# A two-layer graph network: some gathered rows of the second layer become TensorE products, and x passes through DRAM between the layers

## The chip, the cores and the metric

The kernel runs on one core of a Trainium2 chip. The metric is the device time of one execution in microseconds. Engines are named as in the profile: PE is TensorE (PEld its weight loads), DVE is VectorE, ACT is ScalarE, POOL is GpSimd, and SP is SyncE, which here only issues transfers.

## The reference

A graph has 6,250 nodes with 128 features and 200,000 edges, sorted by target node. Two layers are applied, each on the normalised and rectified features, and each is added to x:

```python
h = jnp.maximum(_layernorm(x, axis=-1), 0.0)
x = x + _L0_gnn_ref(h, src, dst, ...)     # attention
h = jnp.maximum(_layernorm(x, axis=-1), 0.0)
x = x + _L1_gnn_ref(h, edge_attr_4, edge_attr_8, ...)   # messages
```

The first layer multiplies h by W, and for every edge takes the row of its source node, a logit per head, a softmax over the edges of each target, and the weighted sum. The second layer multiplies h by `wup` to a table of 128 columns (s and v parts), takes for every edge the table's row of the source node, multiplies it by weights which a small network (8 to 64 to 64 to 128) makes from the edge's features, forms 256 message values and sums them per target; `wout` maps the sums back to 128.

## The kernel before

Edges are cut into 1,563 tiles of 128 edges, one edge per partition. KB = 16 tiles make a block; there are NB = 98 blocks, the last with 11 tiles. Nodes are cut into NX = 50 tiles of 128; a block of edges feeds some 64 nodes, so that a node tile is finished by every second block. A function at run time checks that the targets are even enough, and `even_edges` (line 1008) does the work; `tile_any_edges` is not entered.

**Gathers.** The rows of source nodes come by indirect DMA, one per tile, issued by POOL (`gather`, line 831, issue on line 833): table t0 (136 columns) in the first layer, t1 (128 columns) in the second. A block's rows lie in one buffer `g` of `z_pool`, which has 5. POOL issues them in program order and runs ahead as far as the buffers allow; `take_rows` asks for a block's rows two blocks ahead in the second layer.

**Row transfers.** In blocks 3, 6, 9, ..., 93 (`by_row`) the last tile is not gathered: SP issues 128 transfers of one row each, whose offsets it loads from `at` (`rows_by_row`, lines 1117 to 1133), into one of 3 buffers `r`; `filled` (line 1142) copies it into `g` on ACT. `rows_until` places these transfers in SP's program about three blocks ahead of their use.

**First layer.** For each block DVE, PE and ACT make one-hot matrices, logits, maxima and weights, and PE sums the rows by matrix products (`sums`, line 1284). When a node tile is ended, `node_x` to `node_s` (lines 1298 to 1341) add it to x, normalise and multiply by `wup`, and ACT leaves the table's tile in `sv` (2 buffers). `node_out` (line 1343) stores it from SP to t1 and to t1z, a copy of t1 without the last NL = 3 node tiles. x stays in SBUF, in `x_all`, 50 tiles.

**Change of layers.** The first NE = 24 tiles of the second layer are gathered from t1z, before the last three node tiles are known; PE adds those nodes' rows with one-hot products (`late_ends`, `late_rows`, lines 1658 and 1672). The first gather from t1 waits for the store of the last node tiles.

**Second layer.** A step is 4 tiles. In each, PE does a quarter of the next block's network (`network`, line 1553) and the weights of the next step (`tensor_weights`), DVE forms the messages (`messages`, line 1592, from `vy` to `mj`) and the next one-hot matrix, and PE sums (`sums1`, line 1617). Every second block PE, ACT and DVE finish a node tile (`node1`, line 1625) and SP stores it (`node_out1`). `edge_rows` (line 1545) loads the edge features `ft` and `yb` from SP two blocks ahead. PE, DVE, ACT and SP work in the order of the program; on each of them an instruction that waits holds all behind it.

The one-hot comparison reads the column numbers from PSUM (`held`), where also copies of three columns of `yb` lie, in turn for three blocks.

Of the kernel before, what the change touches and what calls it, by code (L numbers as in the profile page):

```python
# [9 lines left out]
F32 = mybir.dt.float32  # L10
# [731 lines left out]
def tile_even_edges(  # L742
# [88 lines left out]
    def gather(to, table, tiles, width, first=0):  # L831
        for k, t in enumerate(tiles, first):
            nc.gpsimd.indirect_dma_start(  # L833
                out=to[:, k, :width], out_offset=None, in_=table,
                in_offset=bass.IndirectOffsetOnAxis(ap=src_col[:, t : t + 1], axis=0))
        return to
# [171 lines left out]
def even_edges(tc, v):  # L1008
# [8 lines left out]
    with ExitStack() as ctx:  # L1017
        z_pool = ctx.enter_context(tc.tile_pool(name="fz", bufs=5))
        const = ctx.enter_context(tc.tile_pool(name="fconst", bufs=1))
        s_pool = ctx.enter_context(tc.tile_pool(name="fs", bufs=16))  # L1020
        row_pool = ctx.enter_context(tc.tile_pool(name="frow", bufs=3))
        of_l0 = ctx.enter_context(ExitStack())
        l0c = of_l0.enter_context(tc.tile_pool(name="l0c", bufs=1))
# [15 lines left out]
        x_all = const.tile([P, NX, P], F32, name="fx_all")  # L1039
# [3 lines left out]
        identb = l0c.tile([P, P], BF, name="fidentb")  # L1043
        nc.vector.tensor_copy(identb, ident)
# [50 lines left out]
        a3p = const.tile([P, 2, P], F32, name="fa3p")  # L1095
        nc.sync.dma_start(a3p, v["a3p"])
# [4 lines left out]
        wout = const.tile([P, 2, P], F32, name="fwout")  # L1101
        nc.sync.dma_start(wout, v["wout"])
# [5 lines left out]
        with tc.tile_pool(name="fat_ps", bufs=1, space=PSUM) as at_ps:  # L1108
            col = l0c.tile([P, P], F32, name="fcol")
            n = NB - 1  # L1110
            nc.vector.tensor_copy(col[:, :n], v["src_col"][:, KB - 1 : n * KB : KB])
            p_c = at_ps.tile([P, P], F32, name="p_c")
            nc.tensor.transpose(p_c[:n], col[:, :n], ident)
            for i, w in enumerate((ZW, P)):
                nc.vector.tensor_scalar(at[i][:n], p_c[:n], float(4 * w), None, op0=OP.mult)
# [30 lines left out]
        def one_hot(t, m, iota=iota):  # L1146

            s = s_pool.tile([P, 4, P], F32, name="s")
            nc.vector.tensor_tensor(s[:, :m], iota[:, None, :].to_broadcast([P, m, P]),  # L1149
                                    dloc[:, t : t + m].unsqueeze(2).to_broadcast([P, m, P]),  # L1150
                                    OP.is_equal)
            return s

        def finish(b, p_u, width, carry, agg, pool):

            if b % 2 == 0:
                agg = pool.tile([P, MW], F32, name="agg")
            o = agg[b % 2 * WB : b % 2 * WB + WB, :width]
            if carry is None:
                nc.vector.tensor_copy(o, p_u[:WB, :width])  # L1160
            else:
                nc.vector.tensor_add(o, p_u[:WB, :width], carry[:, :width])
            carry = pool.tile([WB, MW], F32, name="carry")
            nc.scalar.copy(carry[:, :width], p_u[WB:, :width])
            return carry, agg

# [5 lines left out]
        with tc.manual_schedule(engines=in_order), \  # L1172
# [116 lines left out]

            def node_rows(i, n):  # L1290
                nc.sync.dma_start(x_all[:, i : i + n, :],
                                  xp[i * P : (i + n) * P].rearrange("(j p) f -> p j f", p=P))

            def with_bias(i, n):
                x_i = x_all[:, i : i + n, :]
                nc.vector.tensor_add(x_i, x_i, bias_b[:, None, :].to_broadcast([P, n, F]))

            def node_x(u):
                i, n, agg = u["i"], u["n"], u["agg"]
                x_i = x_all[:, i : i + n, :]  # L1300
                if n == 1:
                    with_bias(i, n)
                rd = l0n.tile([P, 2, H], F32, name="rd")[:, :n]
                nc.vector.tensor_scalar(rd, agg[:, :n, F:ZW], 1e-9, None, op0=OP.max)
                nc.vector.reciprocal(rd, rd)
                sums_ = agg[:, :n, :F]
                heads = sums_.rearrange("p j (h d) -> p j h d", d=D)
                nc.vector.tensor_mul(heads, heads, rd.unsqueeze(3).to_broadcast([P, n, H, D]))
                nc.vector.tensor_add(x_i, x_i, sums_)
                u["mv"] = moments(l0n, x_i, n, f"n{n}")  # L1310
# [4 lines left out]
            def node_h(u):  # L1315
                i, n = u["i"], u["n"]
                rs, mr = normal(l0n, u["mv"], u["rs"], n, f"n{n}")
                xn = u["xn"] = l0n.tile([P, 2, P], F32, name="xn")
                nc.scalar.activation(xn[:, 0, :], x_all[:, i, :], AF.Identity, bias=mr[:, 0, :],
                                     scale=rs[:, 0, :])  # L1320
                if n == 2:
                    nc.vector.tensor_scalar(xn[:, 1, :], x_all[:, i + 1, :], u["mv"][:, 1, 0:1],
                                            rs[:, 1, :], op0=OP.subtract, op1=OP.mult)
# [19 lines left out]
            def node_out(u):  # L1343
                i, n, sv = u["i"], u["n"], u["sv"]
                first = i * P - W0
                for table in (t1, t1z) if i < LATE else (t1,):
                    if i == 0:
                        nc.sync.dma_start(table[: P - W0, :], sv[W0:, 0, :])
                    else:
                        nc.sync.dma_start(  # L1350
                            table[first : first + n * P].rearrange("(j p) f -> p j f", p=P), sv)

# [59 lines left out]
            rows, rows_until.n, late = rows_by_row(0, t0, ZW), 0, []  # L1412
            for i in range(2):
                node_rows(i, 1)
            for g in range(NG - 3):
# [3 lines left out]
                for n in late:  # L1419
                    node_out(n)  # L1420
                if g % 2 == 0 and g // 2 + 2 < NX - 2:
                    node_rows(g // 2 + 2, 1)
# [10 lines left out]
                maxima(c)  # L1433
                ends_of(n2, 1)
# [33 lines left out]
                late = nodes  # L1468
                if b4:
                    sums(b4, 8)  # L1470
                if g == NG - 4:
                    for q in range(4):
                        ends_of(c1, q)
                    masks_of(c1)
                    for q in range(4):
                        turned(c1, q)
                        er_of(c1, q)
                    er_sum(c1, True)
            node_rows(NX - 2, 2)
            for n in late:  # L1480
                node_out(n)
            with_bias(NX - 2, 2)
# [5 lines left out]
            maxima(c3)  # L1488
            neighbours(c4, c5, c3)
# [26 lines left out]
            (u,) = ended(c4, st)  # L1516
            weighted(c2, 0)
# [22 lines left out]
        with tc.manual_schedule(engines=in_order), \  # L1540
                tc.tile_pool(name="l1", bufs=3) as l1, \
                tc.tile_pool(name="l1n", bufs=2) as l1n, \
                tc.tile_pool(name="l1_ps", bufs=2, space=PSUM) as l1_ps:

# [8 lines left out]
            def network(b, step):  # L1553
# [7 lines left out]
                if step == 3 or 2 * q0 + 8 >= KT[b] and second:  # L1561
                    c["yp"] = held[:, P + b % 3 * KB * 3 : P + (b % 3 + 1) * KB * 3].rearrange(
                        "p (t i) -> p t i", i=3)
                    nc.scalar.copy(c["yp"], c["yb"][:, :, 1:4])  # L1564
# [59 lines left out]

            def node1(i, agg):
                x_i = x_all[:, i, :]
                p_n = l1_ps.tile([P, 4, P], F32, name="p_n", bufs=1)
# [3 lines left out]
                nc.scalar.copy(m_t, p_n[:, :2])  # L1631
                for q in range(2):
                    nc.tensor.matmul(p_n[:, 2, :], m_t[:, q, :], wout[:, q, :], start=q == 0, stop=q == 1)
                nc.vector.scalar_tensor_tensor(x_i, p_n[:, 2, :], POST, x_i, op0=OP.mult, op1=OP.add)
                return i

            def node_out1(i):
                x_i = x_all[:, i, :]
                if i == 0:
                    nc.sync.dma_start(out[: P - W0, :], x_all[W0:, 0, :])  # L1640
# [5 lines left out]
            iota_p = held[:, :P]  # L1646
# [25 lines left out]
            def late_rows(t):  # L1672
                if t < NE:
                    z, k0, oh = blk[t // KB]["z"], t % KB, late_ends.of.pop(t)
                    p_n = l1_ps.tile([P, 4, P], F32, name="p_n", bufs=1)
                    for k in range(4):
                        for j in range(NL):
                            nc.tensor.matmul(p_n[:, k, :], oh[:, j, k, :], sv_late[:, j, :],
                                             start=j == 0, stop=j == NL - 1)
                    z = z[:, k0 : k0 + 4, :P]  # L1680
                    nc.vector.tensor_add(z, z, p_n)
# [6 lines left out]
            def take_rows(b):  # L1688
# [3 lines left out]
                elif b < NB:  # L1692
                    blk[b]["z"] = gathered(t1, range(b * KB, b * KB + KT[b] - (b in by_row)), P)

            rows, rows_until.n, late = rows_by_row(1, t1, P), 0, []
# [9 lines left out]
            us[0]["s"] = one_hot(0, us[0]["m"], iota_p)  # L1705
# [3 lines left out]
            for i, u in enumerate(us):  # L1709
                b, k0, m = u["b"], u["k0"], u["m"]  # L1710
                if k0 == 0:
                    take_rows(b + 2)
                    filled(1, b, blk[b]["z"], P)
                    edge_rows(b + 2)
                if k0 == 4:
# [8 lines left out]
                messages(u)  # L1724
                late_rows(4 * (i + 1))
                if i + 1 < NU:
                    n = us[i + 1]
                    n["s"] = one_hot(n["b"] * KB + n["k0"], n["m"], iota_p)
# [18 lines left out]
            p_n = l1_ps.tile([P, 4, P], F32, name="p_n", bufs=1)  # L1747
# [11 lines left out]
            x_i = x_all[:, NX - 2 :, :]  # L1759
# [140 lines left out]
```

## Time and profile before

| what | value |
|---|---|
| median of 3 runs (lowest to highest) | 3866.83 us (3866.21 to 3874.36) |
| profiled execution, whole | 3867.01 us |
| its span, first to last instruction | 3865.1 us |
| first layer / second layer | to about 1962 us / from there |
| busy share PE, DVE, ACT, POOL | 73, 58, 36, 75% |
| granted PE clock, mean | 0.813 |
| DMA engines busy | about 0.28 in the first layer, 0.24 in the second |

Times within the trace are microseconds from the start of the span. A row of the groups gives line, engine, operation, output and input by name, count, busy time, mean of one in ns, and behind the second bar the idle time of the engine just before such instructions with what ended most of it. In a list in order of time the columns are start, length (of all merged, with their number behind x), engine, line, and in brackets the idle time before with what ended it. "issue" is a time in which the engine waited for nothing that the profile shows.

### The profile page before, as it was taken

What the parts mean: (1) busy time and instruction counts of PE and PEld (TensorE: products, weight loads), DVE (VectorE), ACT (ScalarE), POOL (GpSimd) and SP (SyncE); (2) the same over time, 40 slices, a digit from 0 to 9 for tenths busy, and PEclk for the clock granted to TensorE, in tenths of its full rate; (3) what the DMA queues carried; (4) which work ended last, traced back from release to release, by engine and by line L of the source; (5) the groups of instructions that cost most, each with busy time, mean ns of one, the idle gap of its engine ahead of it and who ended that gap; (6) DMA issues with size and microseconds to landing.
All of it is one profiled execution on the core that took longest, in us unless ns stands there. A gap on an engine that the chain in (4) does not pass through costs nothing. (4 is left out here: it accounts for less than half of the span.)

```text
span 3865.1 us, 62861 instructions
## 1 busy us (share of the span) xinstructions
PE 2825.6 (73%) x14836; PEld 2380.3 (62%) x14836; DVE 2237.5 (58%) x5485; ACT 1403.0 (36%) x3625; POOL 2900.2 (75%) x3074
## 2 busy tenths in 40 slices
PE   4666566666666666666688888888887788888777
PEld 3666566666566656656576666666665666666655
DVE  6555444444444444444457777777766666666666
ACT  3333322232323233322324444444444444444443
POOL 6777777777777777777777777777777777777776
PEclk7676666666666666666689999999999999999999
DMA  6222222222222222222222222222222222222221
GB/s 176 60 64 62 65 64 62 65 64 63 63 64 63 64 62 65 62 64 62 62 60 62 62 62 62 62 63 62 61 63 62 62 62 62 62 61 62 61 61 50
DMA packets 192048, 250.91 MB, mean 65 GB/s; under 512 B 78768, under 2 KB 141872, under 8 KB 191664
## 3 DMA queue, kind: packets, MB, share of 16 engines
q0 software_dynamic: 98048, 207.21, 22.6%
q1 hardware_dynamic: 93184, 39.50, 3.9%
q8 instruction: 120, 1.97, 0.2%
q14 instruction: 264, 2.16, 0.2%
q10 hardware_dynamic: 432, 0.08, 0.0%
HBM read 232.98 MB, written 13.25 MB: 64 GB/s over the span
## 5 line engine op out<-in xcount | busy, mean ns | idle before, releaser
L833 POOL DMA_INDIRECT g<-ft,fsrc x3024 | 2857.7, 945 | 934.4 <-issue 859.1
L1622 PE MATMUL p_u<-mj,s 128*128 128x256 f32 x3126 | 793.6, 398 | 211.2 <-DVE mj L1614 209.8
L1622 PEld LDWEIGHTS p_u<-mj,s 128*128 128x128 f32 x3126 | 591.1, 196 | 379.4 <-DVE mj L1614 303.3
L1286 PE MATMUL p_u<-g,s 128*128 128x136 f32 x3062 | 588.1, 372 | 1.0 <-DVE g L1281 0.4
L1286 PEld LDWEIGHTS p_u<-g,s 128*128 128x128 f32 x3062 | 563.2, 276 | 1.7 <-DVE g L1281 1.6
L1589 ACT ACTIVATE p_w<-p_w,yb 128x64 f32<-128x64 f32 x1563 | 450.3, 288 | 120.5 <-PE p_w L1585 78.8
L1605 DVE TENSOR_TENSOR vy<-g,p_i 128x384 f32<-128x384 f32 x387 | 213.0, 550 | 364.6 <-DMA g<-ft,fsrc 258.1
L1585 PE MATMUL p_w<-fa3p,h 128*128 128x256 f32 x1564 | 412.3, 387 | 0.0
L1203 PE MATMUL p_d<-fident,s 128*128 128x128 f32 x1563 | 370.6, 400 | 0.9 <-DVE s L1149 0.9
L1585 PEld LDWEIGHTS p_w<-fa3p,h 128*128 128x128 f32 x1564 | 289.3, 195 | 117.9 <-issue 51.9
L1228 DVE TENSOR_TENSOR e_s<-g,p_n 128x128 f32<-128x128 f32 x96 | 27.5, 286 | 554.6 <-DMA g<-ft,fsrc 498.1
L1570 ACT ACTIVATE h<-p_h,fb 128x512 f32<-128x512 f32 x196 | 134.7, 687 | 580.2 <-PE p_h L1568 580.2
L1203 PEld LDWEIGHTS p_d<-fident,s 128*128 128x128 f32 x1563 | 300.7, 218 | 11.6 <-DVE s L1149 1.1
L1196 ACT COPY mk<-p_m 128x385 f32<-128x385 f32 (+1 forms) x99 | 47.7, 482 | 701.4 <-PE p_m L1193 693.6
L1281 DVE TENSOR_TENSOR g<-g,pe 128x1024 f32<-128x1024 f32 x193 | 225.5, 1209 | 127.3 <-ACT g L1272 127.3
L1205 ACT CAST d<-p_d 128x512 bf16<-128x512 f32 x391 | 228.2, 586 | 180.4 <-PE p_d L1203 137.2
L1231 PE MATMUL pe<-fident,e_s 128*128 128x128 f32 x98 | 37.7, 384 | 329.9 <-DVE e_s L1229 329.9
L1149 DVE TENSOR_TENSOR s<-p_n,fdloc 128x512 f32<-128x512 f32 x391 | 266.1, 682 | 7.2 <-ACT sv L1341 3.4
L1149 DVE TENSOR_TENSOR s<-p_i,fdloc 128x512 f32<-128x512 f32 x391 | 266.4, 681 | 3.8 <-ACT p_i L1564 3.8
L1568 PE MATMUL p_h<-ft,fa1p 128*128 128x128 f32 x1568 | 215.4, 282 | 67.7 <-DMA ft<-in_e_f_dram 67.7
L1568 PEld LDWEIGHTS p_h<-ft,fa1p 128*128 128x128 f32 x1568 | 209.2, 196 | 88.6 <-issue 72.4
L1575 ACT ACTIVATE h<-p_h,fb 128x512 f32<-128x512 f32 x196 | 134.7, 687 | 304.4 <-PE p_h L1572 304.4
(213 smaller groups left out, 3345.6 us busy)
## 6 DMA issues: line engine op xcount, KB each, us to landing
r<-ft SPq DMA_DIRECT2D x3968, 0.5 KB
r<-ft SPq DMA_DIRECT2D x3968, 0.5 KB
g<-ft,fsrc POOLq DMA_INDIRECT x3024
ft<-in_e_f_dram SPq DMA_DIRECT2D x98, 64.0 KB
yb<-in_e_y_dram SPq DMA_DIRECT2D x98, 32.0 KB
fx_all<-in_e_xp_dram SPq DMA_DIRECT2D x48, 64.0 KB
out_dram<-fx_all SPq DMA_DIRECT2D x47, 64.0 KB
ft<-sv SPq DMA_DIRECT2D x46, 64.0 KB
```

Source lines behind the costliest of these rows:

```text
L833: nc.gpsimd.indirect_dma_start(out=to[:, k, :width], out_offset=None, in_=table, in_offset=bass.IndirectOffsetOnAxis(ap=src_col[:, t : t + ...
L1149: nc.vector.tensor_tensor(s[:, :m], iota[:, None, :].to_broadcast([P, m, P]), dloc[:, t : t + m].unsqueeze(2).to_broadcast([P, m, P]), OP. ...
L1203: nc.tensor.transpose(p_d[:, k, :], c["s"][q][:, k, :], ident)
L1205: nc.scalar.copy(d[:, :m], p_d[:, :m])
L1281: nc.vector.tensor_mul(zh, zh, p_a[:, k0 : k0 + m].unsqueeze(3).to_broadcast([P, m, H, D]))
L1286: nc.tensor.matmul(c["p_u"][:, :ZW], c["s"][k // 4][:, k % 4, :], c["z"][:, k, :], start=c["o"] + k == 0, stop=c["o"] + k == KT[c["b"]] - 1)
L1568: nc.tensor.matmul(p_h[:, q, :], a1p[:, q0 + q, :], c["ft"], start=True, stop=True)
L1570: nc.scalar.activation(c["h1"], p_h, AF.Silu, bias=b1)
L1585: nc.tensor.matmul(w[:, k : k + n].rearrange("p k a u -> p (k a u)"), c["h2"][q // 4][:, q % 4, :], a3p[:, :n].rearrange("p k f -> p (k f) ...
L1589: nc.scalar.activation(w[:, k, ::2, :], w[:, k, ::2, :], AF.Copy, scale=c["yb"][:, k0 + k, 0:1])
L1605: nc.vector.tensor_mul(vy, v_n, y_p)
L1622: nc.tensor.matmul(blk[b]["p_u"][:, :MW], u["s"][:, k, :], u["mj"][:, k, :], start=k0 + k == 0, stop=k0 + k == KT[b] - 1)
```

## The change

In the second layer, the 21 blocks 10, 14, 18, ..., 90 (`dense1`) no longer gather tile 14 (KD). Its rows are made by PE: the table is kept in SBUF as three bf16 parts whose sum is the f32 value (`t1s`, 50 node tiles x 3 x 128), the node numbers of the tile's edges are compared with those of NR = 17 node tiles at once (`dense_ends`: one PE product, two DVE comparisons into the bf16 matrix `ohs`), 51 products are summed in PSUM for three ranges of nodes (`dense_rows`: 12 in each of the last two steps of the block before, 9 in each of the first three of the block itself), and DVE takes the right range for each edge (`dense_taken`, three operations, into the tile's place in `g`).

To make room in SBUF, `x_all` goes. In the first layer a node tile's x and the table's three parts lie in one buffer of 5; DVE makes the parts (`parts`: two casts, two subtractions per tile, one block after the table's tile), and SP stores both in one transfer of 160 KB to `x1` in DRAM (`parts_out`, a block after `node_out`). The last three tiles store x alone. The second layer loads x again per node tile (`node_rows1`, 64 KB) and the parts in 8 transfers, one in each of blocks 0 to 7 (`table_tiles`); the last three tiles' parts come from `sv_late` in SBUF.

With it go: a3p and wout are loaded at the start of the second layer instead of the first; `node1` works in `held`; `yp` alternates between two blocks; the first layer's one-hot matrices have their own pool, the second's a pool of 5; `fcol` lies in a pool of its own; an unused `identb` goes; once, in block 4 of the first layer, `ends_in_ranges` makes the node numbers and range marks for the dense tiles.

```diff
-        x_all = const.tile([P, NX, P], F32, name="fx_all")
...
+        dense1 = set(range(10, NB - 4, 4))
...
+        def in_three(to, of, rest):
+            to = [to[..., k, :] for k in range(3)]
+            nc.vector.tensor_copy(to[0], of)
+            nc.vector.tensor_sub(rest, of, to[0])
+            nc.vector.tensor_copy(to[1], rest)
+            nc.vector.tensor_sub(to[2], rest, to[1])
...
+            def parts(u):
+                i = u["i"]
+                if i < LATE:
+                    rest = l0n.tile([P, P], F32, name="rest", bufs=1)
+                    in_three(parts_of(row_of[i][:, 0]), u["sv"][:, 0], rest)
+            def parts_out(u):
+                i = u["i"]
+                if i < LATE:
+                    nc.sync.dma_start(x1[i], row_of[i][:, 0])
...
+            def node_rows1(i, n=1):
+                x_i = x_of[i] = l1n.tile([P, n, P], F32, name=f"x{n}", bufs=4 if n == 1 else 1)
+                nc.sync.dma_start(x_i, x1[i : i + n, :, :P].rearrange("j p f -> p j f"))
...
+            def table_tiles(b):
+                i = 6 * b
+                if i < LATE:
+                    n = min(6, LATE - i)
+                    nc.sync.dma_start(t1s[:, i : i + n].rearrange("p j s f -> p j (s f)"),
+                                      x1[i : i + n, :, P:].bitcast(BF).rearrange("j p f -> p j f"))
+            def dense_ends(b):
+                p_x = blk[b]["p_x"] = l1_ps.tile([P, 4, P], F32, name="p_x", bufs=1)
+                nc.tensor.matmul(p_x[:, 3, :], key[:, b : b + 1].to_broadcast([P, P]), ident,
+                                 start=True, stop=True)
+                oh = blk[b]["oh"] = l1d.tile([P, NR, P], BF, name="ohs")
+                for k, n in ((0, half), (half, NR - half)):
+                    nc.vector.tensor_tensor(
+                        oh[:, k : k + n], p_x[:, 3:4, :].to_broadcast([P, n, P]),
+                        place_r[:, k : k + n].unsqueeze(2).to_broadcast([P, n, P]), OP.is_equal)
+            def dense_rows(b, k0, n):
+                c = blk[b]
+                for k in range(k0, min(k0 + n, NR)):
+                    i = order[k]
+                    m = len(range(i, NX, NR))
+                    for s in range(3):
+                        nc.tensor.matmul(c["p_x"][:, :m, :], c["oh"][:, k, :], t1s[:, i::NR, s, :],
+                                         start=k == 0 and s == 0, stop=k == NR - 1 and s == 2)
+            def dense_taken(b):
+                c = blk[b]
+                z = c["z"][:, KD, :P]
+                nc.vector.tensor_scalar(z, c["p_x"][:, 0, :], part[:, b, 0:1], None, op0=OP.mult)
+                for r in (1, 2):
+                    nc.vector.scalar_tensor_tensor(z, c["p_x"][:, r, :], part[:, b, r : r + 1], z,
+                                                   op0=OP.mult, op1=OP.add)
+            def dense_step(b, q):
+                if b + 1 in dense1:
+                    if q == 1:
+                        dense_ends(b + 1)
+                    elif q > 1:
+                        dense_rows(b + 1, (q - 2) * 4, 4)
+                if b in dense1:
+                    dense_rows(b, 8 + 3 * q, 3)
+                    if q == 2:
+                        dense_taken(b)
...
                 elif b < NB:
-                    blk[b]["z"] = gathered(t1, range(b * KB, b * KB + KT[b] - (b in by_row)), P)
+                    blk[b]["z"] = gathered(t1, [k for k in range(b * KB, b * KB + KT[b])
+                                                if not (b in by_row and k % KB == KB - 1)
+                                                and not (b in dense1 and k % KB == KD)], P)
...
                     edge_rows(b + 2)
+                    if b % 2 == 0:
+                        node_rows1(b // 2, 1 if b < NB - 2 else 2)
+                    table_tiles(b)
...
                 messages(u)
+                if i == 26:
+                    in_three(t1s[:, LATE:], sv_late, rest)
+                dense_step(b, k0 // 4)
                 late_rows(4 * (i + 1))
```

## The prediction

> **What bounds the kernel now.** I read the page's busy rows first, then the groups, then the gather queue in order of time, then the waits.
>
> ```profile
> PE 2825.6 (73%) x14836; PEld 2380.3 (62%) x14836; DVE 2237.5 (58%) x5485; ACT 1403.0 (36%) x3625; POOL 2900.2 (75%) x3074
> ...
> PEclk7676666666666666666689999999999999999999
> ```
>
> No engine is over 75% busy, and the TensorE clock is 0.65 in the first layer and near full in the second. So the busy shares settle nothing.
>
> ```profile
> L833 POOL DMA_INDIRECT g<-ft,fsrc x3024 | 2857.7, 945 | 934.4 <-issue 859.1
> L1622 PE MATMUL p_u<-mj,s 128*128 128x256 f32 x3126 | 793.6, 398 | 211.2 <-DVE mj L1614 209.8
> ```
>
> POOL's idle time is "issue": it waited for nothing. TensorE waits for messages. In order of time, across the change of layers, the gathers run without a break:
>
> ```profile
> 1956.22 0.94 POOL L833 DMA_INDIRECT fz_first<-ft1z,fsrc  x1 [0.30 <-issue]
> 1957.47 0.94 POOL L833 DMA_INDIRECT g<-ft1z,fsrc  x1 [0.30 <-ACT fsv_late L1341]
> ...
> 1966.20 0.94 POOL L833 DMA_INDIRECT g<-ft1z,fsrc  x1 [0.30 <-issue]
> 1967.45 0.94 POOL L833 DMA_INDIRECT g<-ft,fsrc  x1 [0.30 <-issue]
> ```
>
> One gather starts every 1.249 us (1957.47 to 1967.45 is 8 steps). From 65 us to the last one at 3849.48 there are 3,031 starts, on average 1.2489 us apart, in both layers alike, and 15.6 us of work follow. POOL sets the end.
>
> What stands second? Second layer, waits:
>
> ```profile
> DVE vy L1605 <- DMA g<-ft,fsrc: 258.1, 159, 3.7
> ...
> PE p_h L1568 <- DMA ft<-in_e_f_dram: 67.7, 29, 4.9
> ```
>
> The waits for gathers all fall after 2790 us. The waits of TensorE for `ft` nearly all fall before it. Until then the consumers lag behind the gathers and are paced by SP, whose queue holds the row transfers:
>
> ```profile
> 2035.10 0.37 SPq L1549 DMA_DIRECT2D ft<-in_e_f_dram  x1
> 2035.53 0.42 SPq L1551 DMA_DIRECT2D yb<-in_e_y_dram  x1
> 2036.05 16.41 SPq L1130 DMA_DIRECT2D r<-ft  x44
> 2052.56 0.37 SPq L1549 DMA_DIRECT2D ft<-in_e_f_dram  x1
> ```
>
> SP issues the `ft` of block 3 at 2035.10 and that of block 43 at 2768.68: 18.34 us a block. POOL needs 15.67 x 1.249 = 19.57. So the lag shrinks, by 1.2 us a block. It starts at 34.7 us (block 2 is begun at 2032.06, its gathers ended at 1997.4), and five gather buffers allow about 54 before POOL must stop.
>
> **The change, part by part.** *Removed gathers.* Blocks 10, 14, ..., 90 are 21; each loses one gather: 21 x 1.249 = **26.2 us** off POOL's queue.
>
> *TensorE.* Per dense block 51 bf16 products (48 of 384 columns, 3 of 256), and one f32 product. No row has 384 columns. Nearest: three bf16 products of 512 columns and one of 128, weights reloaded each time, took 0.86 us (L923), the last alone about 0.23, so 0.21 each or 0.41 ns a column: 0.16 us for 384. Four bf16 pairs with 128x128 weights but 24 columns took 0.27 us (L1214), so a weight load adds at most 0.03. Lower end 51 x 0.16 = 8.2 us, upper end (unoverlapped, 0.45 us each as in row L1193) 23. I take 8.8, by the L923 row, plus 0.2.
>
> *VectorE in the second layer.* Two comparisons of 1,152 and 1,024 elements (row L1281, 1,024 in 1.21 us): 2.55; three 128-wide takes, 0.65 back to back. 3.2 us a dense block.
>
> *Does this fit?* Four blocks need 64 - 1.33 (row transfers) - 1 = 61.6 gathers, 76.9 us. The consumers' best pair of blocks (2032.06 to 2065.35) took 33.3, partly waiting for SP; without those waits about 32.3, so 64.6 for four. With 9.0 of TensorE and some 0.5 of VectorE that is not overlapped: about 74. SP: 4 x 18.34 plus two loads of x at 0.47: 74.3. Since each waits for the other in turn, I take 75 for the pair. That is under 76.9, so POOL stays the bound, by only 2.5%.
>
> *What SP gets to wait for.* Each store of x waits for VectorE's parts of that tile; they are made in the block before, ahead of what SP waits for there anyway. `fcol` is copied only after the early rows' last copies, which delays the first row transfer by 0.25 us.
>
> *SP, second layer, once.* Eight loads of the table's parts (576 KB each) and the moved a3p and wout. The 838 KB `fd_q` and 1.5 MB around it landed within 11 us at the start, about 200 GB/s; so a table load lands after some 5 us, while SP tolerates about eight issues (3.3 us) behind an unfinished one. 0.5 to 3.5 us of SP each; I take 2.5, 20 in all, and 4 at the change of layers. This delays `ft` and the rows behind it, so the consumers; the lag at block 10 becomes about 45 instead of 25, still under 54. From there it shrinks by (76.9 - 75)/4 a block, 39 us up to block 90, and by some 3 us a block in the last seven, where SP has no rows left and no dense block comes. It must be down by 57 to cost nothing (in the steady state it is -12); I get 60. So hidden, by little.
>
> *SP, first layer.* 47 stores of 160 KB and one load more or less for the tail. An issue takes 0.4 to 0.5 whatever its size (408 KB: 0.38). SP needs 36.0 us for two blocks (212.6 to 500.6 in eight steps), POOL 39.1; the store makes it 36.5. Its early lag of some 65 us behind the node work now lasts until about 1330 us instead of 1180; POOL does not wait for it, as the first row transfers are late by 10 us and the buffers are freed with 14 us to spare.
>
> *First layer, VectorE.* Two casts and two subtractions for each of 47 tiles, about 0.25 us each, on an engine that is under half busy. The price could lie elsewhere. The Trainium skill ("SBUF — State Buffer", Who interferes with whom) says that VectorE and GpSimd share a port pair by an exclusive lock, which casts within SBUF and operations with two SBUF inputs can take. The trace does show it, for long operations:
>
> ```profile
> 53.38 0.94 POOL L833 DMA_INDIRECT g<-ft,fsrc  x1 [0.30 <-issue]
> 54.63 2.56 POOL L833 DMA_INDIRECT g<-ft,fsrc  x1 [0.30 <-issue]
> 57.50 1.49 POOL L833 DMA_INDIRECT g<-ft,fsrc  x1 [0.30 <-issue]
> ```
>
> ```profile
> 54.49 1.89 DVE L1067 TENSOR_TENSOR feq<-fd_q 128x1664 f32<-128x1664 int32 x1 [10.42 <-DMA fd_q<-in_e_dstt_dram]
> 56.30 1.89 DVE L1070 TENSOR_TENSOR feq<-fd_q,fnxt 128x1664 f32<-128x1664 int32 x1
> ```
>
> Four such operations of 1.9 us cost POOL 3.2 us. By the rule each of 188 new ones could hold it for its length: 188 x 0.25 = 47 us, and the change would lose (3888). But short ones leave no mark: six single-input operations within SBUF at 43.1 to 44.1 fall on gathers of 0.94 and 0.95, and the first layer, with some 240 two-input operations of 0.3 us (L1229, L1296, L1308, L1309), has the second layer's step (1.2490 against 1.2489). I take 0 to 6 us, 0.5.
>
> *Change of layers.* The first gather from t1 (1967.45) needs the late rows' store, issued at 1962.15. Now VectorE does 0.8 us more ahead of it, and a3p, wout and five loads stand in front of it on SP (7 x 0.45). They can go while ScalarE still works on those rows. 0 to 3 us; I take 1.5.
>
> **Sum:** -26.2 + 0.5 + 1.5 + 0.7 for what the lag may leave = -23.5. The profiled execution took 3867.0 (span 3865.1 and 1.9 around it), 0.2 from the median 3866.8. Likeliest: **3843 us**, its own range 3839 to 3850.
>
> **Rivals.**
> *The lag is not recovered* (chance 0.22). If SP and the consumers need 75.8 instead of 75 for four blocks, they win back 20.25 x 1.1 + 21 = 43 of the 57, and 14 us lengthen the tail: 3857; between 75.2 and 76.2, 3845 to 3865. For it: three queues within 3%. [...]
> *The second layer's consumers become the bound* (0.10; the slower side). Place: TensorE's queue in the 21 dense blocks. Price: every microsecond on four blocks costs 20.25 at the end, once the 2.5 of reserve are gone. It is even with before at 76.3, that is with 0.20 us a product instead of 0.17 if none of it is overlapped, and 78 gives 57 - 21 + 22 = 58 us of tail, 3901. For it: TensorE is 83% busy there. Against: the L923 row.
> *The port lock* (0.06): 3870 to 3888, as above.
> *No gain, because the gathers removed were not pacing* (0.03): 3867. The unbroken 1.249 us steps speak against it.
>
> **Numbers.** The likeliest has 0.59. Below 3859.1 is faster by over 0.2% (what this measurement can just tell): 0.59 and just over half of the first rival, 0.71. Within 0.2%: the rest of it, most of the fourth and a little of the second, 0.14. Slower: 0.15. The range reaches from the likeliest's lower end through the first rival: 3838 to 3867.
>
> **What would show it.** Right: 3,003 gathers of this group at 1.249 us steps with no other gap over 1 us; TensorE busier in the second layer by some 190 us of columns; the tail after the last gather near 16 us. Wrong: gathers of 1.1 us and more in the first layer (port), a wait of POOL at 1960 to 2250 (SP's table loads, buffers), a tail of 25 us or more (lag), waits of VectorE for gathers gone altogether (consumers bound).

## The result, and the profile after

The changed kernel took **3843.01 us**, the median of four runs (3841.60 to 3843.57); the kernel before, on the same chip, 3866.52 us (3866.13 to 3874.36). The ratio is 0.9934 with a 95% interval of 0.9917 to 0.9951, so it is faster by 0.66%; by the medians it is 23.5 us, or 0.61%, because one of the four runs before took 3874.36. The profiled execution took 3843.54 us, with a span of 3841.8.

The page of the changed kernel: busy rows, granted TensorE clock, and the two groups that were shown of before.

```profile
PE 2965.8 (77%) x15949; PEld 2484.1 (65%) x15949; DVE 2355.1 (61%) x5805; ACT 1405.7 (37%) x3625; POOL 2880.8 (75%) x3053
...
PEclk7676766666666666666679999999999999999999
...
L834 POOL DMA_INDIRECT g<-ft,fsrc x3003 | 2838.2, 945 | 928.5 <-issue 853.5
L1701 PE MATMUL p_u<-mj,s 128*128 128x256 f32 x3126 | 764.1, 388 | 88.7 <-DVE mj L1693 86.5
```

There are 3,003 gathers instead of 3,024, of the same 945 ns, and their idle time is still "issue". TensorE is busy 140 us longer, and its wait for messages ahead of `p_u` fell from 211.2 to 88.7 us: dense products stand where it used to wait. Part of the fall is the lag's: e1, told below, has no dense product and still waits 139.4 instead of 209.8 us there for VectorE.

The last gather, before and then in the changed kernel:

```profile
3849.48 0.94 POOL L833 DMA_INDIRECT g<-ft,fsrc  x1 [0.30 <-issue]
...
3824.22 0.94 POOL L834 DMA_INDIRECT g<-ft,fsrc  x1 [0.30 <-issue]
```

The last gather starts at 3824.22 instead of 3849.48, so 25.3 us earlier; 17.5 us of work follow it, counted from its start, instead of 15.7. That makes 23.4 us of span. POOL still sets the end.

The waits of the whole execution, for the rows that told the consumers' state before (total us, times, longest):

```profile
DVE vy L1684 <- ACT p_i L1643: 79.5, 94, 3.3
PE p_h L1647 <- DMA ft<-in_e_f_dram: 59.7, 39, 4.9
...
DVE vy L1684 <- DMA g<-ft,fsrc: 21.2, 14, 2.9
```

Before, VectorE waited 258.1 us for gathers in this place (line L1605 there). Now its largest wait here is another one, and 21.2 us in 14 waits are left of it. The consumers (TensorE, VectorE and ScalarE, which work on what POOL gathers) lag behind the gathers nearly to the end. SP's queue shows the pace that they are given. The `ft` of block 11 and that of block 91:

```profile
2195.22 0.36 SPq L1628 DMA_DIRECT2D ft<-in_e_f_dram  x1
...
3684.41 0.37 SPq L1628 DMA_DIRECT2D ft<-in_e_f_dram  x1
```

1489.19 us for 80 blocks are 18.615 a block, 74.46 for four.

A table of the lag (when VectorE begins a block's messages, less when the block's last gather ended, in us; about -13 is the steady state of a kernel whose consumers wait for gathers), worked out from the times of both engines, with the span from the start of the last gather to the end. It takes in the experiments, which are told below.

| kernel | block 10 | 30 | 50 | 70 | 90 | 96 | last gather starts | work after it |
|---|---|---|---|---|---|---|---|---|
| before | 25 | 4 | -12 | -12 | -12 | -13 | 3849.48 | 15.7 |
| after | 43 | 32 | 14 | 3 | -8 | -13 | 3824.22 | 17.5 |
| e1: no dense block | 40 | 20 | -1 | -12 | -12 | -13 | 3851.35 | 17.3 |
| e2: every third block | 43 | 46 | 52 | 55 | 54 | 45 | 3816.24 | 67.6 |
| e3: table loads twice | 59 | 43 | 26 | 15 | 5 | -11 | 3829.54 | 16.2 |
| e6b: one more load a block on SP | 46 | 45 | 39 | 36 | 35 | 19 | 3823.16 | 41.8 |
| e7b: a third more products | 42 | 30 | 15 | 4 | -7 | -13 | 3824.11 | 15.2 |
| e9: one in three, all even | 42 | 36 | 21 | 14 | 3 | -10 | 3814.36 | 15.2 |
| e10: one in four, odd | 40 | 39 | 38 | 37 | 37 | 28 | 3823.75 | 51.1 |

### The profile page after: what moved, and what is told of

Read it like the earlier page. It is cut to its first block, busy times and chain, and to the rows that moved or that the text cites. A ratio compares the mean times of both kernels' runs of the same rounds, so it can differ in the third digit from the quotient of the medians.

```text
span 3841.8 us, 65586 instructions
## 1 busy us (share of the span) xinstructions
PE 2965.8 (77%) x15949; PEld 2484.1 (65%) x15949; DVE 2355.1 (61%) x5805; ACT 1405.7 (37%) x3625; POOL 2880.8 (75%) x3053
## 5 line engine op out<-in xcount | busy, mean ns | idle before, releaser
L1701 PE MATMUL p_u<-mj,s 128*128 128x256 f32 x3126 | 764.1, 388 | 88.7 <-DVE mj L1693 86.5
L1701 PEld LDWEIGHTS p_u<-mj,s 128*128 128x128 f32 x3126 | 581.2, 192 | 216.1 <-DVE mj L1693 139.0
```

What stands on the lines that cost most here:

```text
L1701: nc.tensor.matmul(blk[b]["p_u"][:, :MW], u["s"][:, k, :], u["mj"][:, k, :], start=k0 + k == 0, stop=k0 + k == KT[b] - 1)
```

## The experiments

The theory from the two traces: the 21 gathers are the whole gain; what decides whether it arrives at the end is the lag, and the lag shrinks at the pace that SP's queue allows. The rivals: other edits had a part in the gain; TensorE, not SP, sets the consumers' pace.

**e1: no dense block.** Is the gain that of the gathers?

```diff
-        dense1 = set(range(10, NB - 4, 4))
+        dense1 = set()
```

> The set of dense blocks is empty: all 3,024 gathers are back, the first layer still writes x and the table's parts, the second layer still loads x; the tables are not loaded. Nothing of the output is left out. My theory (the 21 gathers are the gain, the rest costs about 1.5 us on the gather queue): the last gather starts 21 x 1.249 = 26.2 us later, at about 3850.5, the consumers catch up as before near block 40, the tail is back to 15.6, so about 3867 to 3868, that is 0 to 1.5 us above before. Rival (a part of the gain came from the other edits, such as the freed buffers or x kept out of SBUF): clearly under 3863.

Measured: 3868.66 us (3867.02 to 3870.51) against 3867.93 of before on the same chip, ratio 1.000 (0.999 to 1.001). With the gathers back the gain is gone; storing x and the parts and loading both cost 0.7 us by the medians, less than the interval can tell. One sentence of the expectation was wrong: the table's loads do not depend on the dense blocks, so they were still issued. That is why the lag at block 10 is 40 here and not 25. Two more things follow. The lag falls from 40 at block 10 to 6 at block 46, where the gathers take 19.57 us a block; so these blocks took 18.6 us each without a single dense product, just as in the changed kernel with them. SP's queue runs at the same pace too; the `ft` of blocks 11 and 91 in e1 are 18.615 a block apart:

```profile
2195.66 0.36 SPq L1628 DMA_DIRECT2D ft<-in_e_f_dram  x1
...
3684.88 0.37 SPq L1628 DMA_DIRECT2D ft<-in_e_f_dram  x1
```

And the consumers had caught up by block 62, yet 17.3 us follow the last gather: the 1.9 us more at the end of the changed kernel need no leftover lag.

**e3: each table load twice**, the second into a tile that nobody reads. Is the lag really just hidden?

```diff
+            twin = l1d.tile([P, 6, 3, P], BF, name="twin")
...
                     nc.sync.dma_start(t1s[:, i : i + n].rearrange("p j s f -> p j (s f)"),
                                       x1[i : i + n, :, P:].bitcast(BF).rearrange("j p f -> p j f"))
+                    nc.sync.dma_start(twin[:, :n].rearrange("p j s f -> p j (s f)"),
+                                      x1[i : i + n, :, P:].bitcast(BF).rearrange("j p f -> p j f"))
```

> Each load of the table's parts is followed by a second one of the same rows into a tile that nobody reads; nothing of the output is left out. It adds lag in the first dense blocks and no gather. My theory (the lag of the consumers is just recovered by block 94, so new lag comes out at the end): 8 x 1.8 = 14 us of SP, of which POOL may absorb a few by waiting for buffers early; the tail grows from 17.6 to about 30 and the time to 3850 to 3858. Rival (lag hidden with room to spare): 3843 to 3845.

Measured: 3848.41 us (3847.54 to 3849.82), ratio 0.9948 (0.9932 to 0.9965); between the 3843 to 3845 of the rival and my 3850 to 3858, and by another way than mine. The tail was not longer (16.2). The lag rose to 59 at block 10, and POOL had to wait for its buffers, twice. The gather queue's own rows, with the idle time before them:

```profile
2193.62 0.94 POOL L834 DMA_INDIRECT g<-ft,fsrc  x1 [1.12 <-DVE mj L1693]
...
2235.53 0.94 POOL L834 DMA_INDIRECT g<-ft,fsrc  x1 [3.47 <-DVE mj L1693]
```

Less the usual 0.30 of each, that is 4.0 us. The ratios of the two kernels to their own runs of before differ by 0.0014, which is 5.4 us with an uncertainty of several us (by the medians it is 4.0). So the gather buffers cap the lag near 59 us: what goes beyond is paid at once, on POOL. And a lag of 59 at block 10 was worked off by the end. The changed kernel, which starts from 43, had about 16 us to spare, where I had taken its reserve for used up.

**e6b: one more small load a block on SP.** The load of `yb` is issued twice.

```diff
                     nc.sync.dma_start(c["yb"], y4[:, b * KB : (b + 1) * KB, :])
+                    again = l1.tile([P, KB, 4], F32, name="again", bufs=2)
+                    nc.sync.dma_start(again, y4[:, b * KB : (b + 1) * KB, :])
```

> The same kernel as e6, on another chip, because on the chip of that run ScalarE stood still for 10 to 15 us at a time in every kernel and all times were 1.6 times as long. Theory A (SP's queue sets the pace of the consumers): 19.05 us a block instead of 18.615, the lag shrinks by 0.15 a block instead of 0.64, the time is about 3857. Theory B (TensorE sets the pace, SP has room): 3843 to 3845.

Measured: 3867.92 us (3865.83 to 3871.90), ratio 1.0005 (0.9996 to 1.0015). One load of 0.42 us in SP's queue takes the whole gain away. SP's rows of the new load, and the `ft` of blocks 11 and 91 again:

```profile
2198.27 0.36 SPq L1628 DMA_DIRECT2D ft<-in_e_f_dram  x1
2198.74 0.37 SPq L1630 DMA_DIRECT2D yb<-in_e_y_dram  x1
2199.16 0.42 SPq L1632 DMA_DIRECT2D again<-in_e_y_dram  x1
...
3726.97 0.36 SPq L1628 DMA_DIRECT2D ft<-in_e_f_dram  x1
```

19.109 us a block, 0.49 more than in the changed kernel; 76.4 for four blocks against 77.0 of the gathers. The lag shrinks by 11 us in 80 blocks instead of by 51, and 41.8 us follow the last gather, which itself comes no later. Theory A holds. Its time was 11 us short, though the lag at block 90 came out as expected, 35 against 34. I took 23 us to be won back in the last blocks and the 11 that were left for the cost, and forgot that the lag is free only at -13: 34 - 23 + 13 are 24, and the tail is 24.2 longer than in the changed kernel.

**e7b: a third more products in each dense block**, 68 instead of 51.

```diff
                         nc.tensor.matmul(c["p_x"][:, :m, :], c["oh"][:, k, :], t1s[:, i::NR, s, :],
                                          start=k == 0 and s == 0, stop=k == NR - 1 and s == 2)
+                        if s == 0:
+                            nc.tensor.matmul(c["p_x"][:, :m, :], nought, t1s[:, i::NR, s, :],
+                                             start=False, stop=False)
```

> The same kernel as e7 (17 products more in each dense block, with zeros as the weights), on another chip, for the same reason. Theory A (TensorE stands as close to the gather queue as SP): 77.0 us for four blocks against 76.9 of POOL, the lag is not recovered, about 3866. Theory B (SP alone sets the pace, the products are hidden behind it): 3843 to 3846.

Measured: 3840.81 us (3839.66 to 3841.07), ratio 0.9933 (0.9916 to 0.9950), the same as the changed kernel's 0.9934. Theory A falls: 2.7 us more of TensorE in every dense block (its products took 237.3 us between 2200 and 3700 us instead of 182.9) cost nothing. TensorE's own waits in that stretch say where the products went. In the changed kernel:

```profile
PE p_u L1701 <- DVE mj L1693: 53.8, 79, 1.2
PE p_h L1647 <- DMA ft<-in_e_f_dram: 41.2, 32, 2.8
PE p_i L1715 <- ACT m_t L1713: 21.0, 41, 0.6
```

and in e7b:

```profile
PE p_u L1701 <- DVE mj L1693: 49.0, 60, 1.2
PE p_i L1715 <- ACT m_t L1713: 20.9, 41, 0.6
PE p_i L1711 <- DVE s L1152: 12.8, 20, 0.6
PE p_h L1647 <- DMA ft<-in_e_f_dram: 9.1, 11, 1.9
```

32 us of waiting for `ft`, that is for SP, have become products. SP set the pace, and TensorE had room behind it. Its granted clock in this stretch was 0.97 before, 0.96 in e1, and 1.00 in the changed kernel and in e7b; how much of the room comes from that was not tested.

**e2: every third block**, 28 gathers fewer instead of 21.

```diff
-        dense1 = set(range(10, NB - 4, 4))
+        dense1 = set(range(10, NB - 4, 3))
```

> Every third block is dense instead of every fourth: 28 gathers are replaced instead of 21. Nothing of the output is left out. If POOL's gathers alone set the end: 7 x 1.249 = 8.7 us more, 3834. My theory (in the changed kernel the consumers need 4 x 18.615 = 74.5 us per four blocks, and its reserve is used up at block 94): three blocks with one dense take about 18.6 to 19.3 a block against 19.15 to 19.2 of POOL, the lag stays near 40 to 45 us until block 91 and some 25 us are left for the tail: 3855 to 3870; the last gather starts near 3815.5, and the tail after it is over 30 us.

Measured: 3886.09 us (3883.77 to 3891.92), ratio 1.0048 (1.0031 to 1.0065): slower than before, and 16 us above the upper end of what I gave. The last gather starts at 3816.24, as it should. But the consumers took 19.3 us a block, the lag grew from 43 to 54, and 67.6 us follow the last gather. It looked like TensorE at its limit, which e7b contradicts: its 21 times 68 products are as many as the 28 times 51 here. The waits of TensorE in the same stretch show another row on top:

```profile
PE p_u L1701 <- DVE mj L1693: 51.6, 65, 1.2
PE p_i L1711 <- DVE s L1152: 49.7, 26, 3.2
```

L1711 are the node update's transposes, and they wait up to 3.2 us for VectorE (12.8 us in all in the changed kernel, at most 0.6 at a time). In this kernel dense blocks are even and odd by turns, in the changed kernel they are all even. The mean times of six successive blocks, from one start of VectorE's messages to the next, are 23.1, 15.1 (even dense block and the one after), 21.5, 22.6 (the one before an odd dense block, and that block), 17.1 and 16.5. In the changed kernel the four are 23.8, 15.1, 17.8 and 17.8. The node update runs in the second step of every even block. The two comparisons for a dense block run in the second step of the block before it: beside the node update exactly if the dense block is odd. The next two kernels test this.

**e10: one in four, but odd.**

```diff
-        dense1 = set(range(10, NB - 4, 4))
+        dense1 = set(range(11, NB - 4, 4))
```

> 21 dense blocks as in the changed kernel, one in four, but odd: 11, 15, ... 91. Nothing of the output is left out. Theory A (parity): an odd dense block and the one before it take 44 us, as in the every-third kernel, the other two at least 33.7, so 77.7 or more for four blocks against 76.9 of POOL: the lag grows a little, some 35 to 40 us are left at the end, and the time is 3875 to 3890. Theory B (parity makes no difference, SP's 74.5 us for four blocks decide): 3842 to 3846.

Measured: 3877.40 us (3876.66 to 3879.30), ratio 1.0029 (1.0017 to 1.0040), inside the 3875 to 3890 of theory A. The same number of dense blocks, one block later, costs 34 us and turns the gain into a loss. TensorE's largest wait between 2200 and 3700 us, six times what it is in the changed kernel:

```profile
PE p_i L1711 <- DVE s L1152: 75.8, 39, 3.2
```

In order of time, VectorE and then TensorE at one of these places:

```profile
2892.34 2.49 DVE L1784 TENSOR_TENSOR ohs<-p_x,place_r 128x1152 bf16<-128x1152 f32 x2 [0.27 <-PE p_x L1780]
2894.75 0.68 DVE L1152 TENSOR_TENSOR s<-p_i,fdloc 128x512 f32<-128x512 f32 x1
2897.95 0.29 DVE L1716 SCALAR_TENSOR_TENSOR x<-p_i,x 128x128 f32<-128x128 f32 x1 [2.53 <-issue]
```

```profile
2891.92 0.38 PE L1780 MATMUL p_x<-fident,key 128*128 128x128 f32 x2
2895.49 0.69 PE L1711 MATMUL p_i<-fident,agg 128*128 128x128 f32 x2 [3.18 <-DVE s L1152]
2896.64 1.23 PE L1715 MATMUL p_i<-fwout,m_t 128*128 128x128 f32 x4 [0.46 <-ACT m_t L1713]
2897.65 2.77 PE L1701 MATMUL p_u<-mj,s 128*128 128x256 f32 x6
```

The one-hot `s` reads the iota that lies in the PSUM tile `p_i` (which is `held`), and the node update's transposes write that tile. So they wait for `s`, `s` stands behind 2.49 us of comparisons, and the products `p_u` queue behind the transposes. VectorE in turn idles 2.53 us. It is the change that put the transposes into `held`: before, they write a tile of their own, and the trace has no wait ahead of them. The lag stays near 38, since four blocks took 76.8 us, nearly as long as their gathers.

**e9: 28 dense blocks, all even.**

```diff
-        dense1 = set(range(10, NB - 4, 4))
+        dense1 = set(range(10, NB - 4, 6)) | set(range(14, NB - 4, 6))
```

> 28 dense blocks as in the run with every third block, but all of them even: 10, 14, 16, 20, 22, 26, ... 92. Nothing of the output is left out. Theory A (what cost the every-third kernel its gain is the odd dense blocks: their two comparisons fall into the step of the even block before, in which the node update runs, and block 12 took 21.5 us instead of 17.9; TensorE itself has room, as the 17 extra products showed): SP's pace of 18.6 a block holds, POOL needs 19.15, the lag is gone at the end, and the time is 7 x 1.249 = 8.7 us below the changed kernel: 3834 to 3837. Theory B (28 dense blocks are too many for the consumers, whatever their parity): the lag is not recovered, 3860 to 3885.

Measured: **3832.46 us** (3831.57 to 3833.18), ratio 0.9912 (0.9896 to 0.9929), 10.5 us below the changed kernel, 1.5 below what theory A gave, and the fastest of all. The end of its gather queue:

```profile
3814.36 0.95 POOL L834 DMA_INDIRECT g<-ft,fsrc  x1 [0.30 <-issue]
```

9.9 us earlier than in the changed kernel (7 gathers are 8.7), with 15.2 us after it. The blocks keep 18.7 us, the wait for `s` at L1711 is down to 9.0 us between 2200 and 3700, and that for `ft` to 5.1. TensorE now has little left to wait for from SP; whether still more dense blocks would gain was not run.

**e4: the loads of ft and yb from ScalarE's queue.** It was to take 0.85 us a block off SP.

```diff
-                    nc.sync.dma_start(c["ft"], f8[:, b, :])
+                    nc.scalar.dma_start(c["ft"], f8[:, b, :])
...
-                    nc.sync.dma_start(c["yb"], y4[:, b * KB : (b + 1) * KB, :])
+                    nc.scalar.dma_start(c["yb"], y4[:, b * KB : (b + 1) * KB, :])
```

> The loads of ft and yb of the second layer are issued from ScalarE's queue instead of SP's; nothing of the output is left out. My theory: SP paced the consumers; with 0.85 us less on SP a block they run at about 17.7 to 18 us a block, the lag is gone by block 40 to 60 instead of 94, and the end gains only the excess of the tail, 17.6 - 15.6 = 2 us: about 3841. Rival (TensorE and its chain set the consumers' pace, not SP): the pace stays at 18.6 a block and the time at 3843, or a little above from issues on ScalarE.

Measured: 4254.58 us (4245.72 to 4259.20), ratio 1.1001 (1.0982 to 1.1019). A failed experiment: it doesn't bear on SP's pace, because it made new waits. The largest in the second layer, one on VectorE and one on SP's queue:

```profile
DVE x L1716 <- DMA x<-fx: 620.7, 45, 24.9
```

```profile
SPq L1133 <- DMA ft<-in_e_f_dram: 522.4, 90, 13.8
```

By these rows, the row transfers on SP now wait for loads that ScalarE issues late, and the load of x, which stands behind them on SP, comes late for the node update; POOL then waited up to 14.4 us at a time for buffers. Why a row transfer should wait for `ft` was not found out.

**e5 to e8, on another chip.** These four ran on a chip on which the kernel before took 6225.28 us instead of 3867. ScalarE stood still there, mostly for 10 to 15 us at a time, in e5 for example:

```profile
3466.13 0.69 ACT L1654 ACTIVATE h<-p_h,fb 128x512 f32<-128x512 f32 x1 [13.83 <-remote]
```

It was not ScalarE alone: the longest idle time of POOL ahead of a gather that is put down to "issue" was 19.2 us in e5, and 0.3 in the kernel before. Why this chip was slow stays open.

e5 (no dense block, no parts, x alone stored; `dense1 = set()`, no `parts`, no `table_tiles`) was to tell what the parts' casts and subtractions cost the gathers:

> No dense block, no parts of the table (neither the casts and subtractions nor their store nor their loads); the first layer stores only x (64 KB a tile), the second layer loads it. All 3,024 gathers; nothing of the output is left out. My theory (the first layer's gather step of 1.2498 to 1.2501 us, against 1.2489 before, comes from VectorE's casts and subtractions for the parts): the step is 1.2489 again, the first layer 1.3 us shorter than with the parts, and the time 3866.5 to 3867.5. Rival (the step comes from the transfers of x or from the changed code elsewhere): the step stays at 1.2498 or more and the time at 3868 or more. By the lag: without the table loads block 10 is begun some 25 us after its gathers, as before, instead of 40; the lag then shrinks by 1.0 us a block.

It took 6239.59 us, ratio 1.0020 (1.0000 to 1.0039). POOL waits hundreds of us for buffers on that chip, so a difference of 1.3 us can't be read there, and the question stays open. e6 and e7 are the kernels of e6b and e7b:

> In the second layer every block's load of yb is issued a second time from SP, into a tile that nobody reads; nothing else changes and nothing of the output is left out. Each costs SP 0.42 to 0.47 us. Theory A (SP's queue of row transfers and loads sets the pace of the consumers, 18.615 us a block): the pace becomes 19.05, the lag shrinks by 0.15 us a block instead of 0.64, some 34 us of it are left at block 90 and 11 at the end, and the time is about 3857. Theory B (TensorE sets the pace and SP has room): 3843 to 3845.

> Each dense block has 17 products more (68 instead of 51), with a matrix of zeros as the weights, so that nothing changes in the result: 17 x 0.16 = 2.8 us of TensorE in each of the 21 dense blocks. Theory A (TensorE stands as close to the gather queue as SP: 3 blocks of 16.3 and one of 25.3 are 74.2 us): it becomes 77.0 for four blocks against 76.9 of POOL, the lag is not recovered, some 40 us at block 90 and 20 at the end: about 3866. Theory B (SP alone sets the pace, and the products are hidden behind it): 3843 to 3846.

They took 6329.88 (ratio 1.0154) and 6373.80 us (1.0229). e8 put a few more dense blocks at the end:

```diff
-        dense1 = set(range(10, NB - 4, 4))
+        dense1 = set(range(10, 80, 4)) | set(range(81, NB - 4, 3))
```

> Dense blocks every fourth up to 78 and then every third from 81 to 93: 23 instead of 21. Nothing of the output is left out. In the changed kernel the lag is gone by block 80 to 86, and the last seven blocks win back 3 us each, so the end has room for a few more. My theory: the last gather 2 x 1.249 = 2.5 us earlier, the tail not longer by more than 1: 3840.5 to 3842. Rival (every dense block more costs the end what it saves): 3843 to 3848.

6327.87 us, ratio 1.0154 (1.0128 to 1.0180). The sizes that were asked for can't be read from these. One thing can: there the consumers set the pace (in e5 POOL waits 839.5 us for VectorE's messages), and each of the three kernels with dense blocks is 1.5 to 2.3% slower than before; e6 and e7 carry added work, and the changed kernel itself was not run on that chip.

## Why the prediction was right, point by point

**What bounds the kernel.** Right. POOL's 1.249 us a gather set the end before and after; e1 gives the gain back with the 21 gathers.

**-26.2 us.** Right: the last gather came 25.3 us earlier. The rest is, to about 0.1, +1.2 us in the first layer (1,441 steps of 1.2498 us instead of 1.2489 or 1.2490), +0.35 at the start, -0.6 in the stretch of the four long comparisons there, and 0.15 at the change of layers.

**Port contention, 0.5.** Measured 1.2 here, and 0.6 to 1.6 in all the kernels with the parts whose gathers ran without waits (steps of 1.2494 to 1.2501). The first layers of these kernels are alike, so the spread is that of single executions, and of before there is one trace. So it lay inside the 0 to 6. The Trainium skill ("SBUF — State Buffer", Who interferes with whom) has the one that comes second blocked for the whole instruction, from which the prediction worked out 47 us; but it has two-input operations contend only with a GpSimd instruction that reads SBUF, which the prediction left out. The 94 casts alone would be some 22 us by it if each held the lock, an estimate at 0.22 to 0.25 each, and the 1.2 are nowhere near that either. That the casts cost these 1.2 was only argued, since e5 fell on the wrong chip.

**Change of layers, 1.5.** It cost the gathers 0.15. The table loads and the moved a3p and wout delayed the `ft` of block 3 by 3.0 us, not the gather queue.

**Leftover lag, 0.7.** The tail grew by 1.9, but not from lag: the lag was gone (-13 at block 96). Kernels without lag at the end show 15.2 to 17.5 us. In the two long ones the granted TensorE clock in the 10 us around the last gather was 0.91 (changed kernel) and 0.95 (e1); in before, e3, e7b and e9 it was 1.00 there. In the last 13 us it tells nothing: 0.76 in the changed kernel, but 0.79 before. That the clock is the cause was not tested.

**The sum.** +0.5, +1.5 and +0.7 were to take 2.7 off the 26.2. What did was 0.95 on the gather queue and 1.9 in the tail. That the total met the measured time to the tenth is luck: the change of layers was put 1.3 too high, and the tail 1.2 too low.

**Costs of one operation.** The 1,071 products took 188.6 us of TensorE in all (190 predicted), twelve of them 1.95 us; the two comparisons 2.49 (2.55), the three takes 0.35 each, so 1.1 (0.65). A cast took 0.22 to 0.25 and a subtraction 0.29 (0.25 predicted). A table load cost SP some 1.6 us instead of 2.5 (the `ft` of blocks 3 and 11 are 157.1 us apart instead of 143.9; four loads of x are 1.9 of that, seven table loads the rest). The pause comes some eight issues behind a load: after the one at 2038.99 the eighth came 1.97 us after the seventh, where 0.32 is usual. The lag at block 10 was 43 and not 45. SP's 74.3 us for four blocks were 74.46. In the first layer, SP's stores of a tile are 36.3 us apart (36.5 predicted) until about 1400 us (1330).

**"Since each waits for the other in turn, I take 75 for the pair."** This is the step that was wrong, to the safe side. There was no joint pace: SP alone gave it, 74.46 with dense blocks, the same 18.615 a block without any (e1), and only 0.2 more with a third more products (74.65, e7b). "About 74" for TensorE was too high by what it still waited for SP: 41.2 us of `ft` in the 1500 us from 2200 on are some 2 us for four blocks. And four blocks have 61.67 gathers, which are 77.0 us and not 76.9. So the lag fell by 51 up to block 90 and not by 39, and where I wrote "hidden, by little", with 3 us to spare, there were some 16 (e3).

**A reading that was wrong.** Block 2 is not begun at 2032.06, which is the last step of block 1, but at 2035.16. The lag there was 38 and not 34.7. The 25 at block 10, on which the sum rests, was read rightly.

**The lag rival's price** was right, as e6b measured it on purpose: the prediction gives 3865 at 76.2 for four blocks; by the same 20.25 a microsecond, 76.4 is 3869, and 3867.9 came out.

**The slower rival's price** was wrong: "even with before at 76.3, that is with 0.20 us a product". The 68 products of e7b took 11.7 us a dense block, as much as 51 at 0.23, and they cost nothing. The danger was real, but it sat elsewhere. "Some 0.5 of VectorE that is not overlapped" holds for even dense blocks alone. For odd ones the comparisons hold up the node update, the time was 3877.4, and neither the sum nor a rival named that. The prediction didn't compare even blocks with odd ones; that the changed kernel has even ones alone kept it clear of this.

**A sign misread:** waits of VectorE for gathers "gone altogether" were to mean that the consumers had become the bound. They went from 258.1 to 21.2 us although POOL still set the end, because they come only once the lag is gone, and that was near block 90.

## What to carry to other kernels

When one queue sets the end and the others lag behind it, ask how long the lag has to shrink, and by how much each block shrinks it: 0.49 us a block on SP took away 25 us, and 2.7 us on TensorE in every fourth block nothing. Find which of the lagging engines gives the pace before you price its work: look at which one's waits the new work would fill. And when a new step is fitted into a loop whose turns are not alike, look up what else runs in that turn; here the comparisons of 21 dense blocks cost 34 us more in the second step of even blocks, in which the node update runs, than in that of odd ones.

## What was not expected

A small load repeated once a block (0.42 us of SP) costs as much as all 21 gathers gain. The buffers cap the lag: beyond 59 us at block 10, 4.0 us of added lag went straight to POOL and none to the tail. And one chip was met on which all times were 1.6 times as long, with pauses of ScalarE and POOL of 10 us and more that the profile doesn't explain; the three kernels with dense blocks that ran there, two of them with added work, lost against the one before.
